# Four sequences on four bands of the TensorE array in layers 1 and 2

## The chip, the cores and the metric

The kernel runs as one program on one core of a Trainium2 chip. The metric is device time in microseconds (us); the time of a kernel is the median of its timed runs. A separate execution is recorded by the hardware profiler, and all durations below come from that one. Engines are named as in the profile: PE is TensorE's matmuls, PEld its weight loads, DVE is VectorE, ACT is ScalarE, POOL is GpSimd, SP is SyncE, which here only issues DMAs. A line such as L701 is line 701 of the kernel before; the kernel after has other numbers, which are given where they are used.

## The reference

A residual chain of four layers over 32 sequences of 64 tokens with 512 features, all in float32. The change touches layers 1 and 2, both of which add low-rank products that are chosen per sequence:

```python
def _L1_cond_ref(x, W_base, Wt, A, B_w, Wp, scaling, adapter_idx):
    base = jnp.einsum('bsi,oi->bso', x, W_base)
    h = jnp.einsum('bsi,ji->bsj', x, Wt)
    Ab = A[adapter_idx]                      # 4 adapters of rank 16
    Bb = B_w[adapter_idx]
    sc = scaling[adapter_idx]
    z = jnp.einsum('bsj,brj->bsr', h, Ab)
    l = jnp.einsum('bsr,bor->bso', z, Bb)
    return base + jnp.einsum('bso,po->bsp', l, Wp) * sc[:, None, None]

def _L2_cond_ref(x, W, A, Bm, scalings, adapter_idx):
    H = jnp.einsum('btd,od->bto', x, W)
    xa = jnp.einsum('btd,brd->btr', x, A[adapter_idx])   # 8 adapters of rank 16
    delta = jnp.einsum('btr,bor->bto', xa, Bm[adapter_idx])
    return H + delta * scalings[adapter_idx][:, None, None]

x = x + _L0_cond_ref(x, itok_B_1_198, L0_cond_weights)   # one 64x64 matrix per sequence, over tokens
x = x + _L1_cond_ref(...)
x = x + _L2_cond_ref(...)
x = x + _L3_cond_ref(...)   # attention with rotary keys over a paged cache
```

Layer 3 makes queries, keys and values of the tokens, attends over a window of a paged cache and projects.

## The kernel before

The 2048 tokens are worked in 16 tiles of 128 (NT), four tiles to a group, so that there are NG = 4 groups of GT = 512 tokens, or eight sequences each. The kernel merges layers 1 and 2 ahead of time into one matrix of 512 x 512 (mm_s, with both residuals in it) and, for each sequence, 32 ranks: 16 of layer 1 and 16 of layer 2. The weights into the ranks are a_sel[p, chunk, sequence, layer, rank]; the rows out of the ranks, 32 for each sequence, lie in a DRAM table (ranked) and are fetched by gather_ranked(j) with two gathers on POOL's queue into b_sel[j][:, n, :]. Each half n holds the rows of four sequences one below the other, so that sequence q of a half has partitions 32q to 32q + 31.

For a group j the stages are:

- layer0(j): 16 matmuls (L519) give x1T, the tokens turned, as 4 chunks (NC) of 128 features by 512 tokens; ACT copies them out of PSUM.
- ranks(j): for each half, chunk and pair of sequences h, one matmul (L674) with 64 weight columns (two sequences' 32 ranks) and the 128 tokens of both sequences. So each product of a sequence's ranks with the other's tokens is made too, and the two pairs of a half take the lower and the upper 64 partitions of PSUM. Two DVE multiplications (L685) with the mask own then spread the result into z, 128 rows by 512 tokens, with zeros wherever a row's sequence isn't the token's.
- layers12(j): four PSUM banks, one for each output chunk o, take 16 matmuls (L701) with mm_s over all 512 tokens, and then two matmuls each (L711) that add b_sel times z over 128 rows and 256 tokens. ACT copies each bank (L718) into x3T when it is complete.
- both(i), for a tile i: keys and values (L861), queries (L878), the turns of finished queries (L895).

PSUM has eight banks here, handed out in turn by bank(). The order of the work on PE, POOL and SP, and in this part of the kernel on DVE and ACT too, is the order in which it is written. After the set-up it is: layer0(0), layer0(1), ranks(0), layers12(0), ranks(1), layers12(1), both(0) to both(3), layer0(2), both(4) to both(7), ranks(2), layer0(3), layers12(2), ranks(3), layers12(3), both(8) and on, then attention. Between them stand POOL's gathers of cache rows (gather_some, tile old), of ranked rows (b_sel) and of layer-0 weights (w0g), and DVE's search for the owners of cache rows (find_owners, L779 and L787), so that a late stage holds up what is written behind it on the same engine. Layer 0's tokens come by DMA from SP (x0).

Of the kernel before, what the change touches and what calls it, by code (L numbers as in the profile page):

```python
# [8 lines left out]
F32 = mybir.dt.float32  # L9
I32 = mybir.dt.int32  # L10
AF = mybir.ActivationFunctionType
ALU = mybir.AluOpType
# [4 lines left out]
B, T, D = 32, 64, 512  # L17
P = 128
NT = B * T // P
NC = D // P  # L20
# [7 lines left out]
E1, R1, E2, R2 = 4, 16, 8, 16  # L28
# [12 lines left out]
def cond_resid_kernel(  # L41
# [28 lines left out]
    nc = tc.nc  # L70
# [12 lines left out]
    const = ctx.enter_context(tc.tile_pool(name="const", bufs=1))  # L83
# [5 lines left out]
    xs = phase.enter_context(tc.tile_pool(name="xs", bufs=2))  # L89
# [15 lines left out]
    def bank(name):  # L105
        return ps_mm.tile([P, 512], F32, tag="mm", name=name)
# [6 lines left out]
    NG, GT = 4, 512  # L113
# [44 lines left out]
    q_p = part(ALU.logical_shift_right, 5, "q_p")  # L158
# [45 lines left out]
    for h in range(2):  # L204
        rows = slice(h * T, (h + 1) * T)
# [54 lines left out]
    io_e = iota_f([P, R1], [[1, R1]], 0, 0, "io_e")  # L260
# [49 lines left out]
    for w in range(WQ):  # L310
# [5 lines left out]
            op0=ALU.is_equal,  # L316
# [8 lines left out]
    for h in range(2):  # L325
        rows = slice(h * T, (h + 1) * T)
# [63 lines left out]
    for at in range(NC * NC):  # L390
# [3 lines left out]
        if at == 14:  # L394
# [66 lines left out]
    for (name, ne, ii, sb), ep in zip(adapters, (e1_p, e_p)):  # L461
# [10 lines left out]
            op0=ALU.is_equal,  # L472
# [9 lines left out]
    for pick, m, n in ((pick2, masks[1], P), (pick1, masks[0], N1)):  # L482
# [4 lines left out]
            op=ALU.mult,  # L487
# [10 lines left out]
    xTs = {}  # L498
# [36 lines left out]
    for k in range(NC):  # L535
        if k == NC - 1:
# [6 lines left out]
            pa2, lhsT=a2_s[:, k, :], rhs=wb_s[:, k, :], start=k == 0, stop=k == NC - 1  # L543
# [10 lines left out]
        op=ALU.mult,  # L554
# [23 lines left out]
    for k in range(NC):  # L578
# [8 lines left out]
        p12, lhsT=c12T, rhs=pick2.rearrange("p b r -> p (b r)"), start=True, stop=True  # L587
# [5 lines left out]
        op=ALU.mult,  # L593
# [7 lines left out]
    for half in range(2):  # L601
        chunks = range(2 * half, 2 * half + 2)
        picked = {(c, n): bank(f"psel_{c}_{n}") for c in chunks for n in range(2)}
        for c in chunks:
            nc.tensor.matmul(
                picked[c, 1],
                lhsT=m2T[:, c * P : (c + 1) * P],
                rhs=pick2.rearrange("p b r -> p (b r)"),
                start=True,
                stop=False,  # L610
            )
        for c in chunks:
            for n in range(2):
                rows = slice(n * N1, (n + 1) * N1)
                nc.tensor.matmul(
                    picked[c, n],
                    lhsT=m1T[rows, c * P : (c + 1) * P],
                    rhs=pick1[rows].rearrange("p b r -> p (b r)"),
                    start=n == 0,
                    stop=True,  # L620
# [8 lines left out]
        l_i, part_i, 4, 1, op0=ALU.logical_shift_right, op1=ALU.bitwise_and  # L629
# [10 lines left out]
    for q in range(Q):  # L640
        rows = slice(q * 2 * R1, (q + 1) * 2 * R1)
# [5 lines left out]
            op0=ALU.mult,  # L647
            op1=ALU.add,
        )
    own = const.tile([P, Q], F32, name="own")  # L650
    nc.vector.tensor_scalar(own, io_e[:, :Q], q_p, None, op0=ALU.is_equal)
    zs = {}

    def gather_ranked(j):
# [6 lines left out]
                in_offset=bass.IndirectOffsetOnAxis(ap=brow[:, n : n + 1], axis=0),  # L661
            )

    HT = GT // 2

    def ranks(j):


        pz = bank(f"z_{j}")
        for n in range(2):  # L670
            for c in range(NC):
                for h in range(2):
                    b = (n * 2 + h) * 2
                    nc.tensor.matmul(  # L674
                        pz[h * 4 * R1 : (h + 1) * 4 * R1, n * P : (n + 1) * P],
                        lhsT=a_sel[:, c, j * 2 * Q + b : j * 2 * Q + b + 2].rearrange(
                            "p b l r -> p (b l r)"
                        ),
                        rhs=xTs[j][:, c, b * T : (b + 2) * T],
                        start=c == 0,  # L680
                        stop=c == NC - 1,
                    )
        z = xs.tile([P, GT], F32, tag="z", name=f"zs_{j}", bufs=2)
        for n in range(2):
            nc.vector.tensor_tensor(  # L685
                z[:, n * HT : (n + 1) * HT].rearrange("p (h b t) -> p h b t", h=2, t=T),
                pz[:, n * P : (n + 1) * P]
                .rearrange("p (b t) -> p b t", t=T)
                .unsqueeze(1)
                .to_broadcast([P, 2, 2, T]),  # L690
                own.rearrange("p (h b) -> p h b", h=2).unsqueeze(3).to_broadcast([P, 2, 2, T]),
                op=ALU.mult,
            )
        zs[j] = z

    def layers12(j):
        into = x3p.tile([P, NC, GT], F32, name=f"x3T_{j}")
        pls = [bank(f"x3_{j}_{o}") for o in range(NC)]
        for o, pl in enumerate(pls):
            for c in range(NC):  # L700
                nc.tensor.matmul(  # L701
                    pl,
                    lhsT=mm_s[:, c, o * P : (o + 1) * P],
                    rhs=xTs[j][:, c, :],
                    start=c == 0,
                    stop=False,
                )
        for o, pl in enumerate(pls):
            for n in range(2):
                to = slice(n * HT, (n + 1) * HT)  # L710
                nc.tensor.matmul(  # L711
                    pl[:, to],
                    lhsT=b_sel[j][:, n, o * P : (o + 1) * P],
                    rhs=zs[j][:, to],
                    start=False,
                    stop=n == 1,
                )
            nc.scalar.copy(into[:, o, :], pl)  # L718
        xTs[j] = into

    layer0(1)
    for n, quarter in enumerate((0.25, 0.0)):
        if n:
            turns_of(quarter)
            within_half(quarter)
        nc.scalar.activation(trig[:, n].rearrange("p i f -> p (i f)"), red, AF.Sin)
    ranks(0)


# [570 lines left out]
```

## Time and profile before

| what | value |
| --- | --- |
| timed runs, median | 527.42 us (526.8 to 528.32, 3 runs) |
| profiled execution | 499.29 us; span from first to last instruction 497.6 us |
| granted TensorE clock over the span | 0.997 |
| ranks (L674), PE records in all | x128, 7.9 us busy |
| main product (L701) | x128, 55.9 us busy |
| rank-up (L711) | x64, 14.9 us busy |
| copies out of PSUM (L718) | x16, 586 ns each |
| spreading z (L685) | x8, 418 ns each |

A busy time of PE counts each matmul from its start to its modelled end, and those overlap; how long a stage lasted is read from the chain in order of time, where a row has the start in us, the length in us, the engine, the tile and line, and the number of records. In the timeline a row has start, length, engine, line, operation, output and inputs, the array's rows and columns (128*64 is 128 rows by 64 columns), the shape of the moving input, and in brackets the idle time before it and what ended that. In the stretches a row has the stretch, its length, PE's busy time with the number of records, the granted clock, the DMA share and GB/s.

### The profile page before, as it was taken

Reading aid. Unit: us, or ns where it says so; the run is one execution under the profiler, and the core shown is the slowest. Engines: PE = TensorE matmul, PEld = TensorE weight load, DVE = VectorE, ACT = ScalarE, POOL = GpSimd, SP = SyncE. Lnnn points to the kernel's source line nnn. Section 1 sums busy time; section 2 is a strip of 40 time slices with the busy share of each in tenths; the row PEclk is TensorE's granted clock in tenths of the full one; section 3 lists DMA queues with packets and bytes.
Section 4 is the critical chain, followed back from the end, with each engine's and each line's share of the span. In section 5 each row is a group of like instructions: output and inputs, shape, how many; then the busy total and the mean of one; then the engine's idle time right before and its main releaser. Section 6 shows DMA issues by size and latency. Waiting matters only on the chain.

```text
span 497.6 us, 8106 instructions
## 1 busy us (share of the span) xinstructions
PE 485.6 (98%) x2715; PEld 287.3 (58%) x2715; DVE 348.2 (70%) x1096; ACT 235.0 (47%) x624; POOL 220.5 (44%) x234
## 2 busy tenths in 40 slices
PE   7999799999999999999999999999999999999997
PEld 6445645544645664544445666666666766666665
DVE  4783477099776959777658799966767766667671
ACT  2023401123332220323249987766777766677661
POOL 6365157766544554630076744344534434540000
PEclk9999899999999999999999999999999999999999
DMA  5889974988989886798321564454545445530001
GB/s 187 301 262 287 354 238 133 321 261 264 328 253 319 283 285 211 247 295 262 126 63 53 149 165 132 136 166 116 149 129 153 142 121 155 154 116 30 1 22 42
DMA packets 37048, 92.21 MB, mean 185 GB/s; under 512 B 11961, under 2 KB 12985, under 8 KB 36736
## 3 DMA queue, kind: packets, MB, share of 16 engines
q1 hardware_dynamic: 20208, 60.52, 36.9%
q0 software_dynamic: 16512, 30.66, 21.7%
q10 hardware_dynamic: 288, 0.52, 0.3%
q8 instruction: 21, 0.34, 0.3%
q14 instruction: 19, 0.16, 0.1%
HBM read 79.22 MB, written 28.74 MB: 217 GB/s over the span
## 4 chain that ended last, share of the span: by engine, by line
PE 77%; DMA 10%; DVE 5%; ACT 2%; POOL 2%; issue 2%; SPq 0%; POOLq 0%; ACTq 0%
PE pkv L861 11%; PE pq L878 10%; PE pf L1170 10%; PE po L1138 9%; PE ps L1084 8%; PE pp L1122 8%; PE x L701 6%; PE pk L1070 4%; DMA old<-in_cache,at 3%; PE pm L396 3%; DMA b_sel<-ranked,brow 2%; PE x L711 2%; DMA g<-in_qns 2%; PE p L519 1%; PE qT_ps L895 1%
## 5 line engine op out<-in xcount | busy, mean ns | idle before, releaser
L416 POOL DMA_INDIRECT old<-in_cache,at x96 | 93.1, 970 | 85.2 <-issue 21.3
L1010 POOL DMA_INDIRECT kvt<-newkv,new_row x72 | 73.0, 1014 | 92.7 <-PE po L1138 43.4
L1095 DVE CUSTOM_DVE_ANT_0 s<-ps,mk 128x336 f32<-128x336 f32 x128 | 60.8, 503 | 44.1 <-PE ps L1084 43.6
L1105 ACT ACTIVATE s<-s,low 128x336 f32<-128x336 f32 x128 | 73.2, 573 | 22.8 <-DVE low L1095 22.5
L1126 DVE COPY pT<-pp 112x384 f32<-112x384 f32 x128 | 65.0, 550 | 3.8 <-PE pp L1122 3.8
L861 PE MATMUL pkv<-wkv_s,x3T 128*128 128x512 f32 x128 | 57.2, 592 | 0.0
L878 PE MATMUL pq<-wq_s,x3T 128*128 128x512 f32 x128 | 57.2, 592 | 0.0
L1170 PE MATMUL pf<-wo_s,oT 128*128 128x512 f32 (+1 forms) x128 | 56.0, 580 | 0.1
L701 PE MATMUL x<-x1T,mm_s 128*128 128x512 f32 x128 | 55.9, 595 | 0.0
L1084 PE MATMUL ps<-kT,qT 64*128 64x336 f32 x256 | 54.9, 495 | 0.3 <-DVE low L1095 0.3
L1122 PE MATMUL pp<-ident,s 128*112 128x128 f32 x384 | 53.4, 274 | 0.2
L1138 PE MATMUL po<-pT,kvt 112*64 112x128 f32 x696 | 44.6, 277 | 0.0
L1122 PEld LDWEIGHTS pp<-ident,s 128*112 128x112 f32 x384 | 42.4, 133 | 3.6 <-issue 1.6
L878 PEld LDWEIGHTS pq<-wq_s,x3T 128*128 128x128 f32 x128 | 24.2, 190 | 29.7 <-issue 28.9
L701 PEld LDWEIGHTS x<-x1T,mm_s 128*128 128x128 f32 x128 | 24.0, 190 | 29.2 <-issue 29.2
L1138 PEld LDWEIGHTS po<-pT,kvt 112*64 112x64 f32 x696 | 37.6, 137 | 5.1 <-issue 5.1
L1114 ACT ACTIVATE s<-s,tot 128x336 f32<-128x336 f32 x64 | 36.6, 572 | 7.9 <-DVE tot L1112 7.7
L861 PEld LDWEIGHTS pkv<-wkv_s,x3T 128*128 128x128 f32 x128 | 23.7, 190 | 25.9 <-issue 25.8
L718 ACT COPY x3T<-x 128x512 f32<-128x512 f32 x16 | 9.4, 586 | 61.1 <-PE x L711 61.1
L1170 PEld LDWEIGHTS pf<-wo_s,oT 128*128 128x128 f32 x128 | 23.1, 190 | 22.0 <-issue 21.5
L1070 PEld LDWEIGHTS pk<-ident,kvt 112*128 112x128 f32 x174 | 17.2, 140 | 28.4 <-ACT y L1177 5.6
L1084 PEld LDWEIGHTS ps<-kT,qT 64*128 64x128 f32 x256 | 20.1, 184 | 20.1 <-issue 18.5
(230 smaller groups left out, 696.2 us busy)
## 6 DMA issues: line engine op xcount, KB each, us to landing
window<-old SPq DMA_DIRECT2D x29, 672.0 KB, 4.7
kvt<-window SPq DMA_DIRECT2D x29, 672.0 KB, 4.9
x<-in_x SPq DMA_DIRECT2D x16, 256.0 KB, 7.6
newkv<-nk SPq DMA_DIRECT2D x16, 256.0 KB, 7.8
out<-y SPq DMA_DIRECT2D x15, 256.0 KB, 2.0
old<-in_cache,at POOLq DMA_INDIRECT x96, 5.2
kvt<-newkv,new_row POOLq DMA_INDIRECT x72, 3.3
w_s<-in_w2T SPq DMA_DIRECT2D x4, 256.0 KB, 6.1
```

The lines of the kernel that those rows point to most:

```text
L416: nc.gpsimd.indirect_dma_start(out=t[:, c, :], out_offset=None, in_=cache, in_offset=bass.IndirectOffsetOnAxis(ap=rows[:, c : c + 1], axis=0),
L701: nc.tensor.matmul(pl, lhsT=mm_s[:, c, o * P : (o + 1) * P], rhs=xTs[j][:, c, :], start=c == 0, stop=False,)
L861: nc.tensor.matmul(pkv, lhsT=tokens(i, c), rhs=wkv_s[:, c, :], start=c == 0, stop=c == NC - 1)
L878: nc.tensor.matmul(pq, lhsT=tokens(i, c), rhs=wq_s[:, c, :], start=c == 0, stop=c == NC - 1)
L1010: nc.gpsimd.indirect_dma_start(out=kvts[b][:, c, :], out_offset=None, in_=newkv, in_offset=bass.IndirectOffsetOnAxis(ap=rows[c], axis=0), ...
L1084: nc.tensor.matmul(ps[:, :WPOS], lhsT=qTs[b // 2][rows, gp, b % 2].rearrange("p h t -> p (h t)"), rhs=kTs[b][rows, gp, :], start=True, sto ...
L1095: nc.vector.tensor_tensor_reduce(out=s, in0=ps[:, :WPOS], in1=mks[b], scale=1.0, scalar=3.0e38, op0=ALU.add, op1=ALU.min, accum_out=low,)
L1105: nc.scalar.activation(s, s, AF.Exp, bias=low, scale=-1.0, accum_out=tot[:, g2 : g2 + 1])
L1122: nc.tensor.transpose(pp[:KC, c * P : (c + 1) * P], s[:, c * KC : (c + 1) * KC], ident)
L1126: nc.vector.tensor_copy(pT.rearrange("k c q -> k (c q)"), pp[:KC, : 3 * P])
L1138: nc.tensor.matmul(po[g2 * HD : (g2 + 1) * HD, gp, :], lhsT=kvts[b][:, c, (G + g) * HD : (G + g + 1) * HD], rhs=pTs[gp][g2][:, c, :], star ...
L1170: nc.tensor.matmul(pf[:, :n], lhsT=oTs[i][:, c // 2, c % 2].rearrange("p b t -> p (b t)"), rhs=wo_s[:, c, to], start=False, stop=c == NC - 1,)
```

## The change

Each sequence of a half gets a band of its own. In ranks a matmul has one sequence's 32 weight columns and its 64 tokens, and the four sequences of a half take the four bands of 32 columns of the array, that is of PSUM partitions. What lands in PSUM is then what is wanted: row band q holds sequence q's ranks, for the tokens of that sequence in half n. One DVE copy of 128 x 128 brings it out; the mask and its two multiplications are gone.

In layers12 the four PSUM banks are for the bands instead of the output chunks: bank q takes, for all four output chunks, the tokens of sequence q of either half. The main product therefore runs over 128 tokens (two runs of 64) at a time, with the same weights loaded for each bank. The rank-up is one matmul for each half, output chunk and band, with 32 rows and 64 tokens; the band is the innermost loop, and the half the outermost. ACT's four copies stand behind all of it and write x3T in runs of 64 tokens.

```diff
-    own = const.tile([P, Q], F32, name="own")
-    nc.vector.tensor_scalar(own, io_e[:, :Q], q_p, None, op0=ALU.is_equal)
...
         for n in range(2):
             for c in range(NC):
-                for h in range(2):
-                    b = (n * 2 + h) * 2
+                for q in range(Q):
+                    b = n * Q + q
                     nc.tensor.matmul(
-                        pz[h * 4 * R1 : (h + 1) * 4 * R1, n * P : (n + 1) * P],
-                        lhsT=a_sel[:, c, j * 2 * Q + b : j * 2 * Q + b + 2].rearrange(
-                            "p b l r -> p (b l r)"
-                        ),
-                        rhs=xTs[j][:, c, b * T : (b + 2) * T],
+                        pz[q * 2 * R1 : (q + 1) * 2 * R1, n * T : (n + 1) * T],
+                        lhsT=a_sel[:, c, j * 2 * Q + b].rearrange("p l r -> p (l r)"),
+                        rhs=xTs[j][:, c, b * T : (b + 1) * T],
                         start=c == 0,
                         stop=c == NC - 1,
                     )
-        z = xs.tile([P, GT], F32, tag="z", name=f"zs_{j}", bufs=2)
+        zs[j] = xs.tile([P, 2 * T], F32, tag="z", name=f"zs_{j}", bufs=2)
+        nc.vector.tensor_copy(zs[j], pz[:, : 2 * T])
+
+    def layers12(j):
+        into = x3p.tile([P, NC, GT], F32, name=f"x3T_{j}")
+        pls = [bank(f"x3_{j}_{q}").rearrange("p (o n t) -> p o n t", o=NC, n=2) for q in range(Q)]
+        x1T = xTs[j].rearrange("p c (n q t) -> p c q n t", n=2, q=Q)
+        for q, pl in enumerate(pls):
+            for o in range(NC):
+                for c in range(NC):
+                    nc.tensor.matmul(
+                        pl[:, o],
+                        lhsT=mm_s[:, c, o * P : (o + 1) * P],
+                        rhs=x1T[:, c, q],
+                        start=o == 0 and c == 0,
+                        stop=False,
+                    )
         for n in range(2):
-            nc.vector.tensor_tensor(
-                z[:, n * HT : (n + 1) * HT].rearrange("p (h b t) -> p h b t", h=2, t=T),
...
-                op=ALU.mult,
-            )
-        zs[j] = z
-
-    def layers12(j):
-        into = x3p.tile([P, NC, GT], F32, name=f"x3T_{j}")
-        pls = [bank(f"x3_{j}_{o}") for o in range(NC)]
...
-            nc.scalar.copy(into[:, o, :], pl)
+            for o in range(NC):
+                for q, pl in enumerate(pls):
+                    rows = slice(q * 2 * R1, (q + 1) * 2 * R1)
+                    nc.tensor.matmul(
+                        pl[:, o, n],
+                        lhsT=b_sel[j][rows, n, o * P : (o + 1) * P],
+                        rhs=zs[j][rows, n * T : (n + 1) * T],
+                        start=False,
+                        stop=n == 1 and o == NC - 1,
+                    )
+        x3T = into.rearrange("p c (n q t) -> p q c n t", n=2, q=Q)
+        for q, pl in enumerate(pls):
+            nc.scalar.copy(x3T[:, q], pl)
         xTs[j] = into
```

In the kernel after, the ranks' matmuls are on L670, the main product on L689, the rank-up on L700 and ACT's copies of it on L709.

More of the change, by code (lines that the diff above doesn't have):

```diff
@@ L662, in gather_ranked @@
             )
-    HT = GT // 2
     def ranks(j):
@@ L682, in ranks @@
                     )
-        z = xs.tile([P, GT], F32, tag="z", name=f"zs_{j}", bufs=2)
-        for n in range(2):
-            nc.vector.tensor_tensor(
-                z[:, n * HT : (n + 1) * HT].rearrange("p (h b t) -> p h b t", h=2, t=T),
[L687 to L691, printed above, removed]
-                op=ALU.mult,
-            )
@@ L694, in ranks @@
-        zs[j] = z
+        zs[j] = xs.tile([P, 2 * T], F32, tag="z", name=f"zs_{j}", bufs=2)
+        nc.vector.tensor_copy(zs[j], pz[:, : 2 * T])
     def layers12(j):
         into = x3p.tile([P, NC, GT], F32, name=f"x3T_{j}")
-        pls = [bank(f"x3_{j}_{o}") for o in range(NC)]
[L699 to L717, printed above, removed]
-            nc.scalar.copy(into[:, o, :], pl)
+        pls = [bank(f"x3_{j}_{q}").rearrange("p (o n t) -> p o n t", o=NC, n=2) for q in range(Q)]
@@ new lines, in layers12 @@
+        x1T = xTs[j].rearrange("p c (n q t) -> p c q n t", n=2, q=Q)
[9 more added lines that the diff above has]
+                    )
+        for n in range(2):
+            for o in range(NC):
[8 more added lines that the diff above has]
+                    )
```

## The prediction

> **What bounds the kernel now.** I read the page first (busy shares, chain shares), then the chain in order of time, then the timeline and the stretches where two rows had to be set against each other.
>
> ```profile
> PE 485.6 (98%) x2715; PEld 287.3 (58%) x2715; DVE 348.2 (70%) x1096; ACT 235.0 (47%) x624; POOL 220.5 (44%) x234
> ...
> PE 77%; DMA 10%; DVE 5%; ACT 2%; POOL 2%; issue 2%; SPq 0%; POOLq 0%; ACTq 0%
> ```
>
> TensorE is busy nearly always and carries 77% of the chain, so a microsecond taken from it counts, unless something else is then late. The chain in order of time shows where the changed lines stand:
>
> ```profile
> 87.91 7.36 DMA b_sel<-ranked,brow
> 95.41 3.26 PE x L711 x14
> 98.67 3.43 PE pkv L861 x8
> ...
> 162.30 3.57 PE p L519 x32
> 165.87 13.74 PE x L701 x32
> 179.61 3.45 PE x L711 x16
> 183.50 1.90 PE z L674 x32
> 185.39 13.93 PE x L701 x32
> 199.32 3.45 PE x L711 x16
> 202.78 3.43 PE pkv L861 x8
> ```
>
> Two readings. A matmul of the program is two records (16 matmuls of L701 are x32): a float32 product runs in two passes. And groups 2 and 3 are pure TensorE (162 to 203 us), while groups 0 and 1 run into a DMA: the second half of L711 in group 1 starts when b_sel has landed (87.91 + 7.36 = 95.27).
>
> Then the rows that say what packing does:
>
> ```profile
> 35.29 1.00 PE L579 MATMUL pc<-pbT,a_s 128*128 128x64 f32 x8
> ...
> 46.35 1.98 PE L605 MATMUL psel<-pick,m2T 128*128 128x512 f32 x4
> 48.27 1.99 PE L615 MATMUL psel<-pick,m1T 64*128 64x512 f32 x8
> ```
>
> L605 uses all rows: 4 passes in 1.98 us. L615 alternates between two bands of 64 rows: 8 passes in 1.99 us. Two row bands do run at once. Columns likewise: L674 (two column halves) does 32 passes of 128 columns in 1.90 us, L519 (whole array) takes 3.57 us. L579 gives the price of a short pass: 1.00 us less one pass's own length (0.27) leaves 7 gaps of some 0.10 us, though only 64 columns stream; that is hardly better than L519's 128 columns (3.57 / 32 = 0.1116). Loading 128 columns of weights is then the limit.
>
> **The change part by part**, for one group of 512 tokens.
>
> 1. Ranks, L674 (1.90 us). It becomes 32 matmuls (64 passes) of 64 columns on four bands of 32 columns. If four run at once that is 16 slots. A 128-column slot takes 0.109 us (1.74 of the 1.90 us), so a 64-column slot is half of that and a few ns: 0.058. 16 x 0.058 = 0.93, with the switches of shape 1.07 us: -0.83. Bounds: 0.93 us; 2.0 with two at a time; 3.8 one by one.
>
> 2. The main product, L701 (13.74 and 13.93). The same multiplications become 64 matmuls of 128 columns, 128 passes, each with its own load of 128 x 128 weights. That shape has a row, L519: 128 x 0.1116 = 14.28 us, and 0.10 for the first load. With the new switch at its end: +0.64. The input now comes in two runs of 64; no row shows that, I take it at nothing (a gain is excluded, a bubble of 5 ns a pass would cost 0.6 us a group).
>
> 3. Rank-up, L711 (3.45 us: 16 passes of 256 columns, half of each product zeros). It becomes 64 passes of 64 columns on four bands of 32 rows, each with 128 columns of weights. Four at once: 16 slots, and by L579 a slot is bound by the load: 16 x 0.1116 = 1.79, with the switch in and out 2.08: -1.37. Bounds: 1.1 us if short bands load faster, 3.9 with two at a time, 7.1 if loads go singly.
>
> 4. Switches. Between 46.35 and 48.27 lie 1.92 us for four passes of 0.429 (L701: 13.74 / 32): 0.20 for the change of shape, a drain of about 0.09 and one load that nothing hides. Before, a group changes shape twice, now four times; this is inside the sums above.
>
> Sum of a group: -0.83 + 0.64 - 1.37 = -1.56 us. Groups 2 and 3 lie on the path: **-3.1 us**.
>
> A rule of the Trainium skill speaks against the heart of this. "TensorE: Matmul & The Clock Gate", Part 3, The mechanism, says that matmuls start and end strictly in program order, only weight loads being pulled ahead. The two passes of a matmul follow each other on the same band, so in strict order four bands would give pairs at most (second pass of one beside the first of the next). The trace differs: 8 passes of L615 in strict order need five slots (A1; A2 B1; B2 C1; C2 D1; D2) = 5 x 0.429 plus about 0.27 of load and tail = 2.41 us; it took 1.99, four full pairs. So a pass does go past one waiting on another band. By the row the sum is -1.56 a group, by the rule +1.2 (ranks 2.0, rank-up 3.9). That it passes three waiting bands, and that four bands load at once, no row shows; I take it, since nothing in L615 or L674 loses time to either, and give the rest to the rivals.
>
> 5. Groups 0 and 1. Ranks(0) waits for the x1T copies anyway, so it gains 0.6. Rank-up is now ordered half by half over all banks, so the first half of b_sel covers the wait for the second (0.47 us now). Ranks(1) would start at 76.6 instead of 78.8 and the main product of group 1 end near 92.2 instead of 94.3. Its b_sel does not come earlier: those gathers stand on POOL behind others, issued every 1.24 us, and land at about 94.2 and 95.3. So TensorE stands still for 2 us, then does the second half in 0.9 us from 95.35 on; keys and values start at 96.5 instead of 98.5: -2.0.
>
> But an idle TensorE has a price here:
>
> ```profile
> 53.58 5.31 PE L519 MATMUL p<-wd,x 128*128 128x128 f32 x28 [2.68 <-DMA x<-in_x]
> ...
> 52.00:54.00 2.00, 0.42 (x2) 1.00 1.06 388
> 54.00:56.00 2.00, 1.98 (x14) 0.80 1.05 310
> 56.00:58.00 2.00, 2.00 (x12) 0.50 1.05 315
> 58.00:60.00 2.00, 2.00 (x27) 0.85 1.07 395
> ```
>
> After 2.68 us of waiting the granted clock fell to half for (0.20 + 0.50 + 0.15) x 2 / 0.5 = 3.4 us, 1.7 us lost. A new gap of 2 us may or may not do so: cost between 0 and 1.7, I take 1.0. Groups 0 and 1: **-1.0** (from -2.0 to -0.3).
>
> 6. Off the path. DVE: two multiplications by the mask (0.417 each) become one copy of 128 x 128, about 0.28 by its neighbours; it is not urgent, since z is read 14 us later, behind the main product. The mask own (0.23 once) goes. ACT: the four copies (0.586 each; written in runs of 64, as L898 is at 0.377 against 0.366 for L867) can start only after the last rank-up pass, so they end 2.35 us after it instead of 0.6. Cover: after group 1 TensorE takes group 0's tokens, after group 3 group 2's, 27 us of other work; were it gone, the first keys product would wait for two copies, 1.2 us. Eight banks go round, the first of these four is wanted again 7 us later. ACT's next orders (squares of keys) come 3.4 us later. No DMA is added or moved; POOL and SP keep their orders.
>
> Later stages: attention starts on new keys that follow the products, so an earlier TensorE moves it as a whole. In 98.7 to 159.7 us DVE is the nearest limit (50.5 of 61 us busy; the first turned queries are ready at 115.9, TensorE would ask at 117).
>
> Total -3.1 - 1.0 = -4.1 us. The profiled execution took 499.29 us, its span being 497.6 and 1.7 around it; the timed median, 527.42, is 28 us longer for a reason that no record shows. I carry the difference over as it is: 527.4 - 4.1 = **523.3 us**.
>
> **The rivals.**
>
> - Two bands at a time (strict order, or a window too short to look past three waiting bands). Then +1.15 a group: +2.3 in groups 2 and 3, +0.4 in 0 and 1, where the waits for b_sel take up most: **530.1 us**, slower. For it: the rule, and that no row has four bands. Against: L615. It decides from the point where ranks and rank-up together take over 4.7 us a group (1.90 + 3.45 - 0.64); four at once give 3.15, two 5.9.
> - The bands' weight loads go one after another: 64 x 0.107 = 6.9 us of rank-up, about +4.4 a group, +16 in all: **543 us**. Against it: L615's first four loads are started as two pairs 0.1 us apart.
> - Packing works and the gain is lost: a half clock in more than one place, DVE or POOL late next, input runs that cost: **526.5 us**, no change.
>
> **How the numbers follow.** Four at once 0.66, its own range 521.3 (no clock loss, faster loads) to 525.5; lost gain 0.08; two at a time 0.16; single loads 0.10. Under 0.3% (1.6 us) a measurement of this kernel can't be told from no change; the first case lies beyond it, the second within, the last two are slower. The range 521.3 to 530.3 takes the first two and most of the third, and leaves out the single loads.
>
> **What would show it.** Right: z passes (x64) in about 1.1 us, rank-up (x64) in about 2.1, main product (x128) in 14.3 to 14.5, TensorE waiting 1 to 3 us for b_sel before 95 us, then perhaps a stretch with clock 0.5. Wrong: z near 2 and rank-up near 4 us (pairs), rank-up near 7 (single loads), a main product over 15, or keys products after 203 us that start no earlier than now.

## The result, and the profile after

The changed kernel took 549.13 us (median of 4 runs, 545.65 to 550.80); before took 527.87 beside it (526.80 to 530.86): a ratio of 1.0389, 95% interval 1.0336 to 1.0443. The forecast was 523.3 us and its range ended at 530.3, so this lies far outside, on the slow side. The profiled execution of the changed kernel took 549.24 us (span 547.5), like its timed runs. That of before had taken 499.29, unlike its own. Most of what follows is about this difference. Ratios here and below are of fast runs, without those more than 1.5% above the fastest of their kernel, and where a changed kernel had such runs (two of four, the rank-up alone in set B2), its time is that of the others.

The first page lines of the changed kernel, to be set against those of before: busy times of the engines, and the shares of the chain that ended last.

```profile
PE 497.7 (91%) x3419; PEld 323.1 (59%) x3419; DVE 346.9 (63%) x1091; ACT 235.9 (43%) x624; POOL 218.9 (40%) x234
...
PE 77%; issue 7%; DMA 7%; DVE 4%; ACT 2%; another core or an unknown queue 1%; POOL 1%; SPq 0%; POOLq 0%; DVEq 0%
```

TensorE's busy share fell from 98% to 91%, and "issue" rose from 2% to 7% of the chain: time in which an engine of the chain, here TensorE, stands and waits for nothing that the profile records, so for no DVE or ACT instruction and for no DMA.

The chain of waits shows that the packed stages themselves came out about as computed, here in group 3, where no such pause falls (start, duration, what):

```profile
218.05 1.03 PE z L670 x64
219.08 14.49 PE x L689 x128
233.57 1.94 PE x L700 x64
235.51 3.63 PE pkv L852 x8
```

Ranks 1.03 us (before 1.90), main product 14.49 (before 13.93), rank-up 1.94 (before 3.45). The same ranks in group 1 look like this in the timeline (start, duration, operation, passes, idle time before it):

```profile
76.96 0.70 PE L670 MATMUL z<-x1T,a_sel 128*32 128x64 f32 x20
...
81.04 0.33 PE L670 MATMUL z<-x1T,a_sel 128*32 128x64 f32 x2 [1.00 <-issue]
...
92.45 0.13 PEld L670 LDWEIGHTS z<-x1T,a_sel 128*32 128x32 f32 x1 [1.28 <-issue]
...
95.27 0.27 PE L670 MATMUL z<-x1T,a_sel 128*32 128x64 f32 x1 [1.84 <-issue]
...
105.14 0.52 PE L670 MATMUL z<-x1T,a_sel 128*32 128x64 f32 x9 [0.44 <-issue]
```

20 passes run at full pace, then 35 passes take 27 us (78.1 to 105.1), at first two to five and then one at a time, and from 105.14 on they follow each other again, up to 108 us at half the clock. The main product of group 2 has such a stretch from 198.7 to 207.3 us, and attention, whose code was not changed, one of 4.94 us before L1161 at 323.5. So the question was not whether packing works, but what TensorE waits for when "issue" is all that the profile can say.

### The profile page after: what moved, and what is told of

It reads as the page before. It is cut to its first block, busy times and chain, and to the rows that moved or that the text cites. A ratio compares the mean times of both kernels' runs of the same rounds, so it can differ in the third digit from the quotient of the medians.

```text
span 547.5 us, 9508 instructions
## 1 busy us (share of the span) xinstructions
PE 497.7 (91%) x3419; PEld 323.1 (59%) x3419; DVE 346.9 (63%) x1091; ACT 235.9 (43%) x624; POOL 218.9 (40%) x234
## 4 chain that ended last, share of the span: by engine, by line
PE 77%; issue 7%; DMA 7%; DVE 4%; ACT 2%; another core or an unknown queue 1%; POOL 1%; SPq 0%; POOLq 0%; DVEq 0%
PE pkv L852 10%; PE pf L1161 10%; PE pq L869 9%; PE x L689 9%; PE po L1129 8%; PE ps L1075 8%; PE pp L1113 7%; PE pk L1061 5%; PE pm L396 3%; DMA old<-in_cache,at 2%; PE z L670 2%; DMA g<-in_qns 1%; DMA window<-old 1%; PE x L700 1%; PE p L519 1%
## 5 line engine op out<-in xcount | busy, mean ns | idle before, releaser
L1001 POOL DMA_INDIRECT kvt<-newkv,new_row x72 | 71.7, 995 | 106.5 <-PE po L1129 25.8
L689 PE MATMUL x<-x1T,mm_s 128*128 128x128 f32 x512 | 63.0, 285 | 6.9 <-issue 6.8
L689 PEld LDWEIGHTS x<-x1T,mm_s 128*128 128x128 f32 x512 | 61.6, 201 | 7.9 <-issue 7.6
L1161 PE MATMUL pf<-wo_s,oT 128*128 128x512 f32 (+1 forms) x128 | 57.8, 595 | 5.0 <-issue 4.9
L1075 PE MATMUL ps<-kT,qT 64*128 64x336 f32 x256 | 58.6, 506 | 3.2 <-DVE low L1086 3.2
L1113 PE MATMUL pp<-ident,s 128*112 128x128 f32 x384 | 54.6, 277 | 0.6 <-issue 0.4
L709 ACT COPY x3T<-x 128x512 f32<-128x512 f32 x16 | 8.3, 598 | 99.2 <-PE x L700 84.8
L1161 PEld LDWEIGHTS pf<-wo_s,oT 128*128 128x128 f32 x128 | 23.7, 196 | 28.2 <-issue 27.7
L1075 PEld LDWEIGHTS ps<-kT,qT 64*128 64x128 f32 x256 | 21.6, 188 | 24.5 <-issue 19.2
```

What stands on the lines that cost most here:

```text
L689: nc.tensor.matmul(pl[:, o], lhsT=mm_s[:, c, o * P : (o + 1) * P], rhs=x1T[:, c, q], start=o == 0 and c == 0, stop=False,)
L1001: nc.gpsimd.indirect_dma_start(out=kvts[b][:, c, :], out_offset=None, in_=newkv, in_offset=bass.IndirectOffsetOnAxis(ap=rows[c], axis=0), ...
L1075: nc.tensor.matmul(ps[:, :WPOS], lhsT=qTs[b // 2][rows, gp, b % 2].rearrange("p h t -> p (h t)"), rhs=kTs[b][rows, gp, :], start=True, sto ...
L1113: nc.tensor.transpose(pp[:KC, c * P : (c + 1) * P], s[:, c * KC : (c + 1) * KC], ident)
L1161: nc.tensor.matmul(pf[:, :n], lhsT=oTs[i][:, c // 2, c % 2].rearrange("p b t -> p (b t)"), rhs=wo_s[:, c, to], start=False, stop=c == NC - 1,)
```

## The experiments

Kernels of one set ran in turn on one chip, with before among them. What before took in a set turned out to be one of two things, about 500 us or 522 to 532. I call the first kind of set A, the second B; the result above is a B set. All other kernels of a set follow, so a time is only to be read beside the before of its own set.

| set | before | kernel | time | ratio (95% interval) |
|---|---|---|---|---|
| A1 | 501.15 | before once more | 500.45 | 0.997 (0.996 to 0.999) |
| | | main product split | 502.84 | 1.003 (1.001 to 1.005) |
| | | rank-up alone | 496.09 | 0.987 (0.983 to 0.992) |
| | | ranks alone | 498.59 | 0.995 (0.992 to 0.997) |
| B1 | 532.42 | changed | 549.29 | 1.034 (1.027 to 1.041) |
| | | changed, stream shifted | 548.00 | 1.036 (1.027 to 1.045) |
| B2 | 521.67 | before once more | 521.99 | 1.000 (0.997 to 1.002) |
| | | rank-up alone | 540.15 | 1.036 (1.026 to 1.047) |
| | | changed | 542.59 | 1.040 (1.031 to 1.050) |
| A2 | 500.63 | main product split | 501.38 | 1.001 (0.999 to 1.003) |
| | | ranks alone | 498.41 | 0.996 (0.994 to 0.998) |
| | | **changed** | **495.54** | **0.990 (0.987 to 0.993)** |
| | | synthetic streams | 544.55 | |
| A3 | 499.34 | synthetic streams | 547.50 | |
| B3 | 528.38 | b_sel early | 545.66 | 1.034 (1.025 to 1.044) |
| | | synthetic streams | 576.15 | |
| B4 | 527.59 | b_sel early | 544.49 | 1.030 (1.022 to 1.038) |
| | | ranks alone | 538.26 | 1.022 (1.016 to 1.028) |

### One part at a time (set A1)

Before, unchanged.

> The kernel before, unchanged, profiled and timed once more. Its one profile shown so far took 499.3 us while its timed runs took 527. Supply theory (TensorE waits for its own instructions, in the changed kernel more than before): a profile of before near 527 us has some 28 us of idle TensorE that nothing in the profile explains ('issue'), in one or two places, with the clock at half around them; a profile near 499 has none. Bands theory (the packed shapes themselves stall, before is free of it): no such idle time here in either case, and the 28 us lie in longer DMA waits or in the clock. Time expected: 527 (both).

It took 500.45, its profile 500.45 too, without the stall. The set was an A set, so the question of where the 28 us lie had to wait for B2.

Only the main product in 128 columns:

```diff
-                nc.tensor.matmul(pl, lhsT=mm_s[...], rhs=xTs[j][:, c, :], start=c == 0, ...)
+                for s in range(PER):
+                    part = slice(s * P, (s + 1) * P)
+                    nc.tensor.matmul(pl[:, part], lhsT=mm_s[...], rhs=xTs[j][:, c, part],
+                                     start=c == 0 and s == 0, ...)
```

> The kernel before, with only the main product of layers 1 and 2 cut into matmuls of 128 columns: no packing anywhere, but 176 passes (352 TensorE instructions) a group instead of 80 (160). Supply theory: idle 'issue' time of TensorE in layers 1 and 2 as in the changed kernel, 10 to 25 us over before: 537 to 552 us. Bands theory: only the loads that 128 columns do not cover, +0.64 us a group, so +2 us: 529 to 530, no 'issue' time. Chance theory (the stall is set by where block borders of the stream fall, not by how dense it is): anything from 499 to 550, without order by the number of instructions.

502.84, 1.7 us over before: the price of the exposed weight loads (14.49 us a group in its chain, as in the changed kernel), and nothing of the supply theory's 10 to 25 us.

The rank-up on row bands, together with the main product in 128 columns and the banks by band that go with it, but with the old ranks and mask; I call it the rank-up alone. Of its edit, the lines of the rank-up:

```diff
...
-                    lhsT=b_sel[j][:, n, o * P : (o + 1) * P], rhs=zs[j][:, to],
+                    lhsT=b_sel[j][rows, n, o * P : (o + 1) * P],
+                    rhs=zs[j][rows, n * HT + q * T : n * HT + (q + 1) * T],
```

> The kernel before with its old ranks and mask, but the main product in 128 columns and the rank-up in four row bands as after: 256 + 128 + 64 = 448 TensorE instructions a group. Supply theory: close to the changed kernel's 549 (540 to 550), with 'issue' time. Bands theory with the column bands (ranks) at fault: no stall, 527.4 - 0.73 x 2 - 1 = 525; with the row bands at fault: about 549. Chance theory: no order.

496.09, 5.1 us under before. The theories that named a time had put it between 525 and 550 beside a before of 527.

Only the ranks on column bands:

```diff
-                for h in range(2): ...  pz[h * 4 * R1 : (h + 1) * 4 * R1, n * P : (n + 1) * P]
+                for q in range(Q): ...  pz[q * 2 * R1 : (q + 1) * 2 * R1, n * T : (n + 1) * T]
```

> The kernel before with only the ranks on four column bands of the array; z is spread into the old block-diagonal form by the same two masked DVE operations a group; main product and rank-up as before. 128 + 64 + 32 = 224 TensorE instructions a group instead of 160. Supply theory: little more to fetch, so little stall beyond that of before: 524 to 532. Bands theory with the column bands at fault: some 20 us over before, 545 to 550, the stall lying in the ranks of group 1 as in the changed kernel. No stall at all beyond before: 527.4 - 0.83 x 2 - 1 = 525.

498.59, 2.6 us under before. In this set every part did about what the prediction had said of it, or better, and no packed shape stalled.

### The changed kernel again, and shifted (set B1)

> The changed kernel, unchanged, timed again beside before. What is to be told apart: in the last runs before took 501 us, not 527, and with the rank-up alone changed 496. Supply theory (the stall of some 40 us belongs to the changed instruction stream): 520 to 525 us or more beside 501 of before, with the same long 'issue' gap in the ranks of group 1 (78 to 105 us). Surroundings theory (the stall, 28 us of it in before too, belongs to the place or chip where those first runs took place, and not to the kernel): about 495 us, 5 to 7 under before, and no 'issue' gaps; the first forecast of -4.1 us then holds.

> The changed kernel with 56 instead of 24 of the transposes that open TensorE's work (they compute nothing that is used): all later TensorE instructions stand 64 places further on in the stream, so block borders of 256 instructions fall on other work. They cost 32 x 0.107 = 3.4 us of a time in which TensorE waits for its first inputs (a gap of 1.4 us follows them), so +0 to +3 us. Supply theory by block borders: the gap leaves the ranks of group 1 and shows at another place, or is gone: anything between 495 and 550. Supply theory by density: as the changed kernel. Surroundings theory: the changed kernel's time plus 0 to 3 us.

Both at 548 to 549, but before was at 532, not 501. The shift moves every block border of 256 instructions by 64 places, and the stall stayed where it was (again 18 to 21 us of "issue" in L670, in the same microseconds). So the stall is bound to a time in the program, not to a place in the instruction stream; the theory by block borders fell.

### Three kernels side by side (set B2)

> The kernel before, unchanged, run in turn with the changed kernel and with the one that has only the rank-up changed. Twice now before took 527 to 532 us when it was run beside the changed kernel, and once 501 when it was not. Surroundings theory (something outside the kernel, the same for all kernels run at one time, slows them): 527 to 532 here, with some 28 us of idle 'issue' time of TensorE in the profile, which the profile at 499 us has not. If it is 501 here while the changed kernel is at 549: the stall belongs to the changed kernel and the earlier two were chance.

> The kernel with only the rank-up on four row bands (and the main product in 128 columns), run beside the changed kernel. It took 496 us beside a before of 501. Surroundings theory, with a loss that grows with the number of TensorE instructions: before 530, this one 540 to 546, the changed one 549. Surroundings theory with a loss that is the same for all: 524. Theory that only the ranks on column bands stall: 496.

> The changed kernel again, beside the two others. Surroundings theory: either all three are at their lower times (501, 496, about 495) or all three at their higher ones (530, 540 to 546, 549). Theory that the stall belongs to the changed kernel: 549 while the others are at 501 and 496.

All three were high together: before 522, rank-up alone 540, changed 543. The rank-up alone had been 5 us faster than before in A1 and is 18 us slower here, the same program. And before has the stall too. In its timeline:

```profile
84.75 9.28 PE L701 MATMUL x<-x1T,mm_s 128*128 128x512 f32 x21
94.37 1.29 PE L701 MATMUL x<-x1T,mm_s 128*128 128x512 f32 x2 [0.34 <-issue]
97.16 1.29 PE L701 MATMUL x<-x1T,mm_s 128*128 128x512 f32 x2 [1.50 <-issue]
99.97 1.01 PE L701 MATMUL x<-x1T,mm_s 128*128 128x512 f32 x1 [1.52 <-issue]
102.76 1.93 PE L701 MATMUL x<-x1T,mm_s 128*128 128x512 f32 x2 [1.77 <-issue]
```

7 passes in 10.5 us (94.4 to 104.9). In the same 10.5 us the changed kernel got 6 (and 35 in its whole 27 us). A pass of 512 columns is 0.43 us of work, one of 64 columns on four bands 0.016, so what runs short is counted in passes and not in work. I read that as a shortage of instructions. It also fits that before reaches the stretch late, at 94.0 us, while the packed kernel was dry at 77.7: long passes use up a stock of instructions more slowly.

That it is instructions is a reading, though, and one record speaks against the simplest form of it. The instructions of TensorE come in packets of 16 KB that the profile lists (queue q8: 21 packets for the 2715 passes of before, 27 for the 3419 of the changed kernel). In the changed kernel one such packet came between 76 and 79 us, in 0.9 us, and none from 78.2 to 113.8; in before (B2) one came between 88 and 90 us and none from 89.6 to 142. So while passes came singly no packet was under way. They and those after them ran without a further one, and whatever holds them up does so when their packet has come.

### Shapes and traffic apart: synthetic streams (sets A2, A3, B3)

A kernel that runs one stream of TensorE work four times: first without other traffic, then beside 24 loads of 1 MB by SP, then beside 72 gathers by POOL with 24 stores of 672 KB by SP, then without again.

```diff
+    def work():
+        whole_array(8, D)
+        bands_of_columns(16)
+        whole_array(8, P)
+        bands_of_rows(16)
```

That is 64 passes of 512 columns, 1024 in the shape of the packed ranks, 256 of 128 columns and 1024 in the shape of the packed rank-up.

> A synthetic kernel that computes nothing of the reference and writes a constant: after 8 banks of 512-column matmuls it runs four times the same TensorE stream: 256 passes of 512 columns (by the rows of the profile 110 us... 8 banks x 4 matmuls x 2 passes x 0.429 = 27.5 us), 1024 passes of four column bands (16.5 us), 256 passes of 128 columns (28.6 us), 1024 passes of four row bands (31 us). First without other traffic, then beside 24 loads of 1 MB by SP, then beside 72 gathers by POOL and 24 stores of 672 KB, then without again. Bands theory: the stretches of bands are slow (over 20 and 40 us) in all four rounds. Instruction supply by itself: the dense stretches lose in all rounds, 512 columns in none. Instruction supply hindered by traffic: rounds one and four as computed, 'issue' gaps in the second or third, most where instructions are densest (column bands: 2048 of them in 16.5 us), few in the 512 columns. If none loses: something of the kernel that this one lacks.

(The first stretch is 64 passes, which is what its 27.5 us were worked out from, not the 256 that the expectation names.) Set A2, without traffic; the timeline of TensorE, and the packets of its instruction queue over the whole run:

```profile
64.44 1.99 PE L111 MATMUL b<-xt,w 128*32 128x64 f32 x128 [1.34 <-issue]
68.17 1.99 PE L111 MATMUL b<-xt,w 128*32 128x64 f32 x128 [1.74 <-issue]
71.63 1.99 PE L111 MATMUL b<-xt,w 128*32 128x64 f32 x128 [1.46 <-issue]
...
87.13 28.85 PE L124 MATMUL b<-xt,w 128*128 128x128 f32 x256
115.92 28.81 PE L139 MATMUL b<-xt,w 32*128 32x64 f32 x1024
...
q8 instruction: 74, 1.21, 0.9%
```

Here a shortage of instructions can be seen in the clear. The work comes in pieces of 128 passes, that is 256 instructions (each pass is a load and a multiplication), 1.99 us of work and then 1.3 to 1.7 us of "issue". 74 instruction packets for 9566 passes are one for 129 passes, of 16.4 KB each. So TensorE was fed 128 passes in some 3.6 us; column bands want them in 1.99, while row bands (3.60 us for 128 passes) were just fed and passes of 128 columns (14.4) easily. Beside the loads a piece came every 6.2 us. Beside the gathers row bands lost as well: 47.9 us (363.94 to 411.87) instead of 28.8, most of it at half clock after two short waits.

> The synthetic streams again, unchanged. If before is at 501 beside it: as in the first run (column bands: 128 passes in 1.99 us and then 1.4 to 1.7 us of waiting in the rounds without traffic, 5.5 to 6.2 us for 128 passes beside loads or gathers; 128 columns at 28.8 us and row bands at 28.8 us undisturbed except beside gathers). If before is at 520 to 532: supply theory says that blocks come later, so column bands take well over 6 us per 128 passes and passes of 128 columns and row bands stall too, at least beside traffic; if the streams are as in the first run, the supply is not what differs.

Set A3: the same, but for the column bands beside the gathers, which took 40.0 us (298.15 to 338.13) against 36.4 in A2 (298.76 to 335.16).

> The synthetic streams a third time. If before is at 501: as twice. If before is at 520 to 532: supply theory expects blocks of 128 passes in well over 3.7 us without traffic or over 6 us with, and stalls also in passes of 128 columns; if the streams are as before, the supply as measured here is not what differs.

Set B3, before at 528. Without traffic (1.99 and 1.46 us) and beside the loads (a piece in 5.9 to 6.5 us) the streams were as in A2. Beside the gathers they were not: the 1024 passes of column bands, 36.4 and 40.0 us in the A sets, took 91.4 (296.47 to 387.88). Lines of TensorE's timeline there, and then POOL's own in the same microseconds, those with a pause of over 2 us:

```profile
301.02 0.27 PE L111 MATMUL b<-xt,w 128*32 128x64 f32 x1 [1.17 <-issue]
301.72 3.08 PE L111 MATMUL b<-xt,w 128*32 128x64 f32 x105 [0.43 <-issue]
305.01 0.43 PE L111 MATMUL b<-xt,w 128*32 128x64 f32 x4 [0.21 <-issue]
...
316.68 3.09 PE L111 MATMUL b<-xt,w 128*32 128x64 f32 x88 [0.45 <-issue]
320.08 0.46 PE L111 MATMUL b<-xt,w 128*32 128x64 f32 x6 [0.31 <-issue]
...
326.75 2.35 PE L111 MATMUL b<-xt,w 128*32 128x64 f32 x76 [1.01 <-issue]
```

```profile
303.65 0.93 POOL L173 DMA_INDIRECT old<-in_cache,at  x1 [3.88 <-DMA window<-old]
...
318.03 0.93 POOL L173 DMA_INDIRECT old<-in_cache,at  x1 [2.33 <-DMA window<-old]
...
327.95 0.93 POOL L173 DMA_INDIRECT old<-in_cache,at  x1 [2.22 <-DMA window<-old]
```

POOL paused from 299.8 to 303.7, 315.7 to 318.0 and 325.7 to 327.9 us, and in each pause, 1 to 2 us after its start, TensorE gets a burst of 76 to 105 passes. The five later bursts of over 50 passes stand in pauses of 1.6 to 3.6 us in the same way; a pause of 1.5 us, up to 312.3, brought none. While POOL issues gathers back to back, it gets 1 to 6 passes a time. SP's stores are being issued all the while (275.7 to 390.2 us), pause or not, so what goes with the held-up passes is the gathers. That they are the cause rests on this coincidence: no run took them away or spread them, and POOL's issuing is not told apart from the data that the gathers move. The 8 instruction packets of this stretch took no longer than the others (0.9 to 1.1 us).

The kernels fit. POOL issues gathers back to back (0.93 us each, 0.30 between) from about 75 us until 101.3 in the changed kernel, 102.0 in before (B2), 109.3 in the rank-up alone (B2); the stretch of single passes ends at 105.1, 104.9 and 111.7. The run of gathers from 190.0 to 205.2 us in the changed kernel is the stretch that ends at 207.3, and the one from 310.7 to 322.5 ends with L1161 at 323.5, where DMA is far from full (68 GB/s from 290 to 330 us). In the later attention, where gathers come in threes with pauses of about 6 us, no stretch follows. But not every run of gathers does it: beside the 12 from 280.7 to 296.1 us in the changed kernel TensorE's passes follow each other until 295.4 (it then waits 3.15 us for DVE), and in A1's before POOL issues the gathers of 75 to 100 us at the same pace, 0.93 us each and 0.30 between, and TensorE loses nothing.

### Parts beside the changed kernel again (set A2)

> The main product in 128 columns and nothing else, beside the changed kernel. It took 503 us beside a before of 501. If surroundings are again those of the higher times (before 520 to 532): loss by the number of TensorE instructions (352 a group against 448 and 512): 535 to 545, with 'issue' gaps in the main product; loss by packed bands: 524 to 533, two over before. If surroundings are the lower ones: 503.

> Only the ranks on four column bands, 224 TensorE instructions a group against 160 before, beside the changed kernel. It took 498.6 us beside a before of 501. In the surroundings of the higher times: loss by the number of instructions: 2 under to 6 over before; loss by packed column bands: 10 to 20 over before. In the lower ones: 498.

> The changed kernel as the measure of the surroundings, fourth time. If the kernels that run in turn with it decide (three times it was there, three times before was slow; once it was not, and before was quick): about 545, before 520 to 532. If it is chance: about 495 beside a before of 501 is as likely.

This was an A set, and the changed kernel is in it at 495.54, 5.1 us or 1.0% under before. So its company does not decide between A and B, and neither does the chip: A1 and B1 ran on the same one. The split took 501.4, the ranks alone 498.4, as in A1. The changed kernel gains no more here than the rank-up alone did there (5.1 us both); the intervals are too wide to say whether the 2 us of the ranks are lost on the way.

### b_sel earlier, and the ranks alone (sets B3, B4)

What remains in A2 is a wait for b_sel in groups 0 and 1. POOL stands idle from 52.5 to 65.9 us while the indices for it are there at 52.7:

```diff
-        gather_some(1)               # end of the loop over half
+        if half == 0:
+            gather_some(1)
...
+    gather_ranked(0)
+    gather_ranked(1)
+    gather_some(1)
     layer0(1)
```

(The two old calls of gather_ranked go.)

> The changed kernel with both gathers of b_sel for groups 0 and 1 issued on POOL before the gathers of old rows that wait for a buffer (POOL stands idle from 52.5 to 65.9 us; the rows of ranked and their indices are there from 52.7 us), and those old rows after them. b_sel then lands at about 60 instead of 75.7 and 95.5 us. In the quick surroundings the changed kernel loses 2.2 + 1.4 us before the rank-up of group 0, 0.8 before that of group 1, and about 1.7 to a half clock after it (keys product 5.33 instead of 3.63 us). If these are on the path: 495.5 less 3 to 6, so 489.5 to 492.5 beside a before of 501 (ratio 0.978 to 0.984). If the old rows, now later on POOL, are late next: 495 to 499. In the other surroundings: 535 to 548 beside 520 to 532.

> The changed kernel with the gathers of b_sel issued early, a second time (the first fell beside a before of 528 and took 546). If before is at 501: 489.5 to 492.5 if the waits for b_sel and the half clock after them are on the path, 495 to 499 if the old rows are late in their place. If before is at 520 to 532: about 545 again.

Twice a B set. The wait for b_sel did go (in B4 the rank-up of group 0 follows the main product at once, at 73.81 us), but TensorE ran dry right there and through the ranks of group 1, and the ratio to before is about the changed kernel's (1.034 and 1.030 against 1.034 to 1.040). What it does in an A set was not measured.

> Only the ranks on four column bands (224 TensorE instructions a group, before 160, the changed kernel 512). If before is at 501: 498.4 again, 0.5% under it. If before is at 520 to 532: supply theory puts the loss at the number of instructions in the stretches beside gathers, so -2 to +6 us to before, far less than the 14 to 24 us of the two kernels with 448 and 512; theory that packed column bands lose as such: 10 to 20 us over before.

538.26, 10.7 us over before; the supply theory, as I had counted it, gave at most 6, and the theory that packed column bands lose as such gave 10 to 20. By instructions a group (224 against 448 and 512) the loss should be small. The timeline shows why it isn't, and why it isn't the column bands alone:

```profile
77.59 0.96 PE L674 MATMUL z<-x1T,a_sel 128*32 128x64 f32 x44
...
87.60 0.27 PE L674 MATMUL z<-x1T,a_sel 128*32 128x64 f32 x1 [1.15 <-issue]
88.32 0.30 PE L674 MATMUL z<-x1T,a_sel 128*32 128x64 f32 x1 [0.45 <-issue]
90.42 1.01 PE L696 MATMUL x<-x1T,mm_s 128*128 128x512 f32 x1 [1.81 <-issue]
91.85 1.01 PE L696 MATMUL x<-x1T,mm_s 128*128 128x512 f32 x1 [0.42 <-issue]
```

The 64 short passes of group 1 stand right in the run of gathers. They use up in 1 us what had been fetched ahead, and from 79 to 90.4 us TensorE gets 20 passes, 0.3 us of work; only then come the long ones, on the whole array, and they come singly too, 6 up to 102.0 us. What fits is not the sum of instructions but how many short passes fall into such a stretch; no further run tried that.

What stays open: what makes a set A or B (all kernels of a set share it; chip and company do not decide it), what holds the passes up when their packet has come, and by which path single ones still get through. That spreading the gathers would cure it was not tried.

## Why the prediction was wrong, and where it was right

The steps for one group were right. They are read in A2 and A1, where before has no such stall; the chain of the changed kernel (A2):

```profile
182.72 1.06 PE z L670 x64
183.78 14.49 PE x L689 x128
198.27 1.94 PE x L700 x64
200.22 3.63 PE pkv L852 x8
```

- Ranks (step 1): -0.83 forecast; 1.90 became 1.03 and 1.06, -0.86 on average. Four column bands run at once.
- Main product (step 2): +0.64 forecast; 13.73 and 13.93 became 14.29 and 14.49, +0.56. The input in two runs of 64 cost nothing, as assumed: the split, with one run of 128, took 14.29 and 14.49 too.
- Rank-up (step 3): -1.37 forecast; 3.45 became 1.94, -1.51. Four row bands and their loads run at once; single loads would have taken 7 us.
- Sum of groups 2 and 3: -3.1 forecast, -3.6 in these lines (19.08 to 17.26 and 19.28 to 17.49). The forecast's 2.08 for the rank-up has the switch of shape behind it in it, which the profile puts into the next row: the keys product took 3.63 instead of 3.43, the turns after group 2 0.59 instead of 0.44. With both the sum is -3.3.
- Groups 0 and 1 (step 5): between -2.0 and -0.3, -1.0 taken. The keys product started 2.2 us earlier (97.67 against 99.89) but then took 5.33 instead of 3.43, because the clock fell, some 2 us after the wait for b_sel. Columns: stretch, its length, PE busy, granted clock, DMA share, GB/s.

```profile
96.00:98.00 2.00, 2.00 (x61) 1.00 0.98 331
98.00:100.00 2.00, 2.00 (x4) 0.54 0.87 287
100.00:102.00 2.00, 2.00 (x5) 0.60 0.69 228
```

  That leaves -0.3, the end of the range with the full price of the clock. The way there was not quite the forecast's: both halves of group 1's rank-up ran in one piece after 0.79 us of waiting (2.06 us from 95.62), and the long waits for b_sel came in group 0 (2.23 and 1.37 us; 2.80 and 2.02 in before, A1). Nor does one trace of each settle the size: against the first trace of before, whose keys product ended at 102.10, the changed kernel's end at 103.00 is 0.9 us later.
- Total: -4.1 forecast, -5.1 measured in A2 (-6.7 to -3.6 by the interval).

The rule weighed there ("TensorE: Matmul & The Clock Gate", Part 3, The mechanism) would have had pairs by the forecast's estimate, ranks of 2.0 and a rank-up of 3.9 us; 1.03 and 1.94 say four, in every stage that no pause disturbs. The estimate also took it that the two passes of a matmul stand next to each other in the program, and no trace here shows their order, so it is the estimate of pairs that is refuted, and the rule only if that holds. The row L615 was the better guide.

The step that failed is the last sentence of the sum: that the timed median is 28 us longer than the profiled execution "for a reason that no record shows. I carry the difference over as it is". It was no constant. The time of before in B sets has TensorE standing in "issue" and getting its passes singly; in A sets, and in the one trace that the forecast had, it has not. The first keys product in the chains of before in A1 and B2, then of the changed kernel in A2 and in the result:

```profile
99.89 3.43 PE pkv L861 x8
110.99 3.43 PE pkv L861 x8
...
97.67 5.33 PE pkv L852 x8
124.13 3.63 PE pkv L852 x8
```

Before lost 11.1 us up to there and 19.5 in all (spans 518.2 and 498.7). The changed kernel, which issues 512 instead of 160 TensorE instructions a group, lost 26.5 us up to the same point and 52.4 in all (547.5 against 495.1). A loss that counts passes was carried over to a kernel with 3.2 times the passes in these stages as if it were a length of time. The passes of layers 1 and 2 are not all of it: up to the end of group 3 the losses are 11.1 and 35.3 us (215.09 against 203.99; 235.51 against 200.22), and the other 8.4 and 17.1 fall into later work that the change left as it was; why that differs is not known. What should have given pause was there: the number of passes in the first page line (x2715 before), and an unexplained difference 7 times as large as the gain to be forecast.

No rival of the forecast had this mechanism. The two on the slow side were about bands (two at a time, single loads), and the traces refute both; the measured time lies beyond both for another reason. (The sum for single loads also came out too high: with the forecast's own ranks and main product it is -0.83 + 0.64 + 3.45 = +3.3 a group, not +4.4.)

The Trainium skill has the block ("Runtime: NRT & Kernel Launch", Instruction fetch mechanics: instructions come in blocks of 16 KiB or 256, fetched ahead), and the pieces of 128 passes agree with it. It also calls the crossing of a block mostly hidden. That holds here for passes of 128 columns (28.85 us for 256 without a gap) or of 64 columns on row bands, and not for 64 columns on four column bands (1.3 to 1.7 us bare per block without any traffic).

## What to carry to other kernels

Count TensorE's passes as well as its microseconds. A change that swaps a few long matmuls for many short ones can gain in one set of runs (1.0% here) and lose several times that in another (3.4 to 4.0%), so time it in several sets, each beside before, and look which stretch the short passes fall into; here it was that of POOL's long runs of gathers. And when the profiled execution and the timed runs of a kernel differ by much more than the change is worth, the difference has a cause that the change may multiply: take it as an unknown of the range, not as a constant.

## What the runs showed of the hardware

- Four bands of 32 rows or of 32 columns run at once: 128 passes of 64 columns took 1.99 us on column bands and 3.60 us on row bands; 128 passes of 128 columns on the whole array, twice the columns, took 14.4.
- Passes of 64 columns on column bands were fed in pieces of 128, one in about 3.6 us without other traffic and one in about 6 us beside loads that move 420 GB/s.
- While POOL issued gathers back to back, TensorE got, in B sets, one to six passes at a time: in the kernels 0.7 to 1.3 a microsecond over 10 to 27 us, and in the synthetic stream bursts of 58 to 129 in each pause of POOL of 1.6 us or more. No instruction packet was under way in the kernels' stretches.
- The profile has no releaser for this: it says "issue". A half clock goes with it (0.50 from 78 to 108 us in the changed kernel), so the loss is longer than the "issue" time.
